# Regrouping the first transfers of a decoder layer: log-decay weights first, decay spreads ahead of the context

## The chip, the cores and the metric

The kernel runs on one core of a Trainium2 chip. The core has a matrix engine (TensorE, PE in the profile, with its weight loads listed as PEld), a vector engine (DVE), an activation engine (ScalarE, ACT), a general engine (GpSimd, POOL) and SyncE (SP), which here only issues transfers. Sixteen DMA engines move data between device memory (HBM) and the core's memory (SBUF); transfers are issued by SP and by ACT. Matrix products land in PSUM, eight banks of which the kernel uses in rotation. The metric is device time in microseconds (us), the median of several executions. One execution was profiled.

## The reference

A post-norm decoder layer on 4 sequences of 1024 tokens with 256 features, in float32, after each of three parts a residual sum and a layer norm:

```python
x = layernorm(x + mamba2(x))             # 16 heads of 16 channels, state 64
x = layernorm(x + cross_attention(x, ctx, mask))   # 16 heads, 77 context tokens
x = layernorm(x + ffn(x))                # 256 -> 1024 -> relu -> 256
```

Inside `mamba2`, for each head, with x the head's 16 channels of the input:

```python
logA = W_logA @ x + b_logA                # one number a token and head
X, Bm, Cm = silu(W_XBC @ x + b_XBC)       # 16, 64 and 64 channels
cum = cumsum(logA)
Y[i] = sum over j <= i of exp(cum[i] - cum[j]) * (Cm[i] . Bm[j]) * X[j]
out = ((W_gate @ x + b_gate) * Y) @ W_out.T + b_out
```

The log-decay weights and biases of the change are `W_logA` and `b_logA`. The context is `ctx`, from which keys and values of the cross attention are made once.

## The kernel before

**Units and stages.** The 4096 tokens are cut into 16 units of 256, each of two chunks of 128. For every unit there are stage A (the Mamba part, with a running state from chunk to chunk inside a sequence), stage B (cross attention) and stage C (the feed-forward part). Every stage is cut into small named jobs. Each job has a place, a number in units of time, from the table `WHEN` or, for units 0, 1 and 15, from `EDGE`. Setup jobs (`s_x`, `s_l`, ...) have places in `WHEN` alone. All jobs are sorted by place and their instructions are issued in that order (L1186 to L1189). Each engine takes its own instructions strictly in this order, so a job that must wait holds up everything behind it on its engine, and a transfer that must wait holds up later transfers of the same issuing engine.

**The opening.** `s_x` (L274) clears the tiles of unit 0's transposed input (`xts[0]`) and of the B and C weights (`w_bc`), and loads them: four slices of `xt` through SP (`load_t`, L248), four slices of `w_bc` and its row of biases through ACT. Then it loads `xu`, a second layout of the transposed input (`load_u`, L240), `w_all` (weights of X, gate and log-decay together) in two halves and the log-decay biases `b_l` in two pieces. `s_l` copies the log-decay columns out of `w_all` into `w_l`; `s_bc` halves `w_bc`; `s_g` loads the X biases and builds `w_x` and `w_g` on GpSimd; `s_x2` and `s_z` clear more tiles there.

`s_c` (L380) loads what the context's keys and values need: `ctxT`, `v_w`, `k_w` (through `packed`, L361, with two GpSimd copies after the load), `v_b`, `k_b` (two loads), the mask twice, and then clears `vz`, the tile of the values, on GpSimd. `s_b` (L403) loads the gate's biases `b_g` in eight small transfers. All of these are issued by SP.

**Unit 0's Mamba part.** `pl` (L585) multiplies `xu` by `w_l`; `cum` (L596) is the running sum over it, with `b_l` as the other operand. `cd` and `ce` (L603, L608) write `cum` to device memory. `dl00`, `dl01`, `dl10` and `dl11` (L616, chunk and half of the heads) read it back, spread over all 128 partitions, 512 KB each: the decay spreads. `ncum` is the negative sum, turned. `ex` (L785) makes exp(cum[i] - cum[j]) on ACT, `sel` (L794) clears the part above the diagonal on GpSimd. `de` (L757) needs both spreads of its chunk.

`pb` (L658) computes B and C on PE, with `xt` and `w_bc`; `th` (ACT) and `bct` (DVE) apply silu; `pg` (L804) is their product on PE, and `st` (L816) multiplies it by the decays on DVE. `px`, `zx`, `thx` and `xz` make X. `pgt` and `gT` (L691, L700) make the gate; `gT` is on ACT and adds `b_g`. `values0` to `values3` (L494) multiply the context of one sequence by `v_w` on PE and add `v_b` into `vz` on DVE.

**The order around the change.** On PE, unit 0 starts with `pb0`, `pl`, `pb1`, `pcum`, `px0`, `pg10`, `px1`, `pgt`, `values0`, then unit 1's `pl` and unit 0's `pg00`, `pg01`. On DVE: the `w_l` copies, the halving of `w_bc`, `bct00`, `cum`, `bct01`, `ncum`, `bct10`, `zx0`, `de0`, `zx1`, `values0`, `xz0`, `bct11`, `st00`. On ACT: its loads, then `th00`, `th01`, `th10`, `th11`, `thx0`, `ex00`, `gT`, `ex01`. On GpSimd: the `b_l` copy, `w_x`, `w_g`, `b_x`, the clears, the copies of `k_w`, the clear of `vz`, `sel00`. On SP: `xt`, `xu`, the loads of `s_c`, `cd`, `ce`, unit 1's `xu`, `dl00`, `dl01`, the loads of `s_b`, `dl11`, `dl10`, then `w_out` in eight pieces.

Of the kernel before, what the change touches and what calls it, by code (L numbers as in the profile page):

```python
# [27 lines left out]
XW = 2 * 64 + 4  # L28
# [5 lines left out]


WHEN = {
    "s_x": -9.9872, "s_l": -9.7484, "s_bc": -8.5276, "s_g": -7.5874, "s_x2": -7.2899,
    "s_z": -5.7593, "s_c": -5.7019, "load_u1": -4.4177, "s_b": -4.0720, "values0": -2.9817,
    "load_u": -2.4239, "pl": -1.9203, "cum": -1.8712, "keys": -1.8678, "s_o": -1.7725,
    "cd": -1.7336, "load_k0": -1.7122, "px1": -1.6221, "ce": -1.5871, "load_t": -1.5843,  # L40
    "values3": -1.5780, "px0": -1.5183, "zx1": -1.5153, "zx0": -1.4952, "pcum": -1.4739,
# [30 lines left out]

EDGE = {
    0: {
        "pb0": -7.2560, "pl": -6.8550, "th00": -6.7669, "bct00": -6.5564, "pb1": -6.2530,
        "cum": -6.1547, "pcum": -5.4565, "th01": -5.3112, "px0": -5.0843, "bct01": -5.0527,
        "cd": -4.9994, "th10": -4.5740, "ce": -4.4923, "ncum": -4.4350, "pg10": -4.3960,
        "dl00": -4.2803, "dl01": -4.2382, "px1": -4.1255, "bct10": -3.8577, "pgt": -3.7592,
        "zx0": -3.6494, "dl11": -3.4590, "de0": -3.3490, "zx1": -3.3017, "th11": -3.2657,
        "thx0": -3.2139, "xz0": -2.9448, "pg00": -2.9088, "bct11": -2.8309, "ex00": -2.7127,  # L80
        "sel00": -2.6115, "dl10": -2.5547, "pg01": -2.3769, "gT": -2.2848, "st00": -2.2420,
        "ptb0": -2.2172, "ex01": -1.9849, "dex0": -1.9659, "bk01": -1.8438, "ec": -1.7085,
        "thx1": -1.7034, "bk00": -1.6781, "de1": -1.5887, "xw0": -1.5820, "sel01": -1.5457,
        "st01": -1.4409, "pc0": -1.2430, "xz1": -1.2245, "ex10": -1.0895, "sn0": -0.9938,
# [87 lines left out]
def decoder_layer_kernel(ctx: ExitStack, tc: tile.TileContext, a: dict, out: bass.AP):  # L172
# [13 lines left out]
    nc = tc.nc  # L186
# [9 lines left out]
    def tile_(shape, tag, name, bufs=2):  # L196
        return sb.tile(shape, F32, tag=tag, name=name, bufs=bufs)
# [17 lines left out]
    xts = [const.tile([P, G, T], F32, name=f"xt_{i}") for i in range(2)]  # L215
# [3 lines left out]
    w_l = const.tile([P, 2, 2 * CH], F32, name="w_l")  # L219
    w_all = const.tile([P, 2, XW], F32, name="w_all")  # L220
    b_x = const.tile([P, 2, 2, 4 * CH], F32, name="b_x")
    b_g = const.tile([P, 2], F32, name="b_g")
    b_l = const.tile([P, 1], F32, name="b_l")
# [16 lines left out]
    def load_u(u):  # L240
        xu = tile_([P, 2, T], "xu", f"xu_{u}", bufs=3)
        nc.sync.dma_start(
            out=xu,
            in_=a["xT"][0:64, :, u * T : (u + 1) * T].rearrange("x (k a) t -> a x k t", a=2),
        )
        xus[u] = xu

    def load_t(u, rs=range(4)):  # L248
        for r in rs:
            nc.sync.dma_start(  # L250
                out=xts[u % 2][32 * r : 32 * r + CH],
                in_=a["xT"][CH * r : CH * r + CH, :, u * T : (u + 1) * T],
            )
# [11 lines left out]
    def setup(name):  # L265
        def put(fn):
            setups.append(name)
            jobs.append((WHEN[name], len(setups) - 100, name, fn))

        return put  # L270

    xgl = a["w_xgl"].rearrange("x (k a) c -> x a k c", a=2)

    @setup("s_x")  # L274
    def _():
        nc.vector.memset(xts[0], 1.0)
        nc.vector.memset(w_bc, 0.0)
        for r in range(4):
            load_t(0, [r])
            own = slice(NS * (r % 2), NS * (r % 2) + NS)  # L280
            nc.scalar.dma_start(
                out=w_bc[32 * r : 32 * r + CH],
                in_=a["w_bc"][CH * r : CH * r + CH, :, :, r // 2, own],
            )
        nc.scalar.dma_start(
            out=w_bc[CH::32], in_=a["w_bc"][64].rearrange("g b q (n s) -> (q n) (g b) s", n=2)
        )
        load_u(0)
        nc.vector.memset(b_l, 0.0)
        nc.vector.memset(w_l, 0.0)  # L290
        for half in range(2):
            nc.scalar.dma_start(out=w_all[64 * half : 64 * half + 64], in_=xgl[0:64, half])
        for k in range(2):
            nc.scalar.dma_start(
                out=b_l[32 * k : 32 * k + 8],
                in_=xgl[64:65, :, k, 128:XW].rearrange("o a r -> r a o"),
            )
        nc.gpsimd.memset(w_x, 0.0)
        nc.gpsimd.memset(w_g, 0.0)
        make_identity(nc, ident)  # L300
        nc.gpsimd.tensor_copy(b_l[64:128], b_l[0:64])

    @setup("s_l")
    def _():
        for half in range(2):
            rows_ = slice(64 * half, 64 * half + 64)
            nc.vector.tensor_copy(
                w_l[rows_, :, 0:8].rearrange("x k (r a) -> x a k r", a=2)[:, half],
                w_all[rows_, :, 128:XW],
            )  # L310
# [876 lines left out]
    with tc.manual_schedule():  # L1187
        for _, _, _, fn in jobs:
            fn()  # L1189
# [77 lines left out]
```

## Time and profile before

Three executions took 698.11, 698.94 and 698.80 us: a median of 698.8. The profiled execution took 698.22, of which its span, from the first to the last instruction, is 696.5 us.

| | busy us | share of the span |
|---|---|---|
| TensorE matmul | 663.4 | 95% |
| TensorE weight load | 526.4 | 76% |
| VectorE | 554.2 | 80% |
| ScalarE | 410.6 | 59% |
| GpSimd | 276.6 | 40% |

| event of the opening | us from the span's start |
|---|---|
| first copy into `w_l`; second | 13.68; 14.64 |
| first matmul (`pb0`) | 15.32 |
| first activation (`th00`) | 18.26 |
| `cum` of unit 0 | 20.09 |
| `cd` issued; `dl00` and `dl01` issued | 20.53; 22.17 to 24.12 |
| `values0` on TensorE | 26.23 to 27.26 |
| second half of `de0` | 33.35 |
| `st00` | 36.09 |

In the lines that follow, "engine line waited for" lists give the waiting engine and line, what ended the wait, the total in us, how many times, and the longest. Lines of the timeline give the start, the length, the engine, the source line, the operation, out<-in, and in brackets the engine's idle time before it and what ended it. ACTq and SPq are the sequencers of ACT and SP, which issue transfers. In the line of a stretch stand its bounds and length, the busy time of PE, PEld, DVE, ACT and POOL with the numbers of instructions, the granted clock of TensorE, the busy share of the DMA engines, and GB/s.

### The profile page before, as it was taken

The numbers are of one execution on the slowest core, as the hardware profiler recorded it, in microseconds if no ns is written. First come the engines' busy times: TensorE is split into PE (matmuls) and PEld (weight loads), VectorE is DVE, ScalarE is ACT, GpSimd is POOL, SyncE is SP. The second block draws the span as 40 slices with busy tenths as digits, with TensorE's granted clock in tenths as the row PEclk, the third lists the DMA queues.
The fourth block names the chain that finished last, engine by engine and source line by source line (L and its number), as shares of the span: only waits on it lengthen the run. The fifth ranks groups of instructions, "written<-read, shape, count | busy, mean of one in ns | idle before, by whom it ended". The sixth has DMA issues, their size and how long they took to land.

```text
span 696.5 us, 19937 instructions
## 1 busy us (share of the span) xinstructions
PE 663.4 (95%) x7968; PEld 526.4 (76%) x7968; DVE 554.2 (80%) x1336; ACT 410.6 (59%) x1091; POOL 276.6 (40%) x448
## 2 busy tenths in 40 slices
PE   1689999999999999999999999999999999999996
PEld 0466777878878787887878788787878788787785
DVE  1388899688888798979888788988878897887653
ACT  0476896647485674838566683837658483853210
POOL 0443445243435354334443435435434443533222
PEclk9988999999999999999999999999999999999999
DMA  4375547032232303223230423223130331100001
GB/s 113 95 182 173 182 142 236 23 114 79 77 122 63 116 22 120 88 85 122 85 108 22 155 85 113 93 85 114 52 119 33 119 95 62 48 1 17 16 1 46
DMA packets 40440, 63.08 MB, mean 91 GB/s; under 512 B 6095, under 2 KB 29340, under 8 KB 40348
## 3 DMA queue, kind: packets, MB, share of 16 engines
q1 hardware_dynamic: 38880, 61.40, 28.5%
q8 instruction: 63, 1.03, 0.6%
q10 hardware_dynamic: 1468, 0.41, 0.3%
q14 instruction: 29, 0.24, 0.1%
HBM read 55.50 MB, written 6.29 MB: 89 GB/s over the span
## 4 chain that ended last, share of the span: by engine, by line
PE 90%; DVE 4%; DMA 3%; SPq 1%; ACT 0%; issue 0%; POOLq 0%; POOL 0%; DVEq 0%
PE pf L1162 17%; PE ph L1135 16%; PE pg L811 9%; PE pb L666 5%; PE pe L1044 5%; PE pa L1069 4%; PE po_a L942 4%; PE pq L972 4%; PE py L915 4%; PE po_b L1105 4%; PE pm L997 3%; PE py L854 2%; PE ptb L832 2%; PE pc L869 2%; PE px L728 2%; PE pgt L695 2%
## 5 line engine op out<-in xcount | busy, mean ns | idle before, releaser
L789 ACT ACTIVATE dl<-dl,ncum 128x128 f32<-128x128 f32 x512 | 156.1, 397 | 8.0 <-DVE de L761 8.0
L797 POOL TENSOR_SCALAR_AFFINE_SELECT dl<-dl 128x1024 f32<-128x1024 f32 x64 | 69.9, 1103 | 136.4 <-ACT dl L789 136.4
L1162 PE MATMUL pf<-w,hT 128*128 128x256 f32 x512 | 122.8, 385 | 0.0
L1135 PE MATMUL ph<-T_c,w 128*128 128x256 f32 x512 | 121.6, 383 | 0.0
L1055 ACT ACTIVATE es<-pe,mb 77x512 f32<-77x512 f32 x128 | 76.9, 679 | 59.2 <-PE pe L1044 58.1
L1135 PEld LDWEIGHTS ph<-T_c,w 128*128 128x128 f32 x512 | 93.9, 190 | 18.0 <-issue 5.4
L1162 PEld LDWEIGHTS pf<-w,hT 128*128 128x128 f32 x512 | 93.0, 190 | 14.3 <-issue 2.1
L821 DVE TENSOR_TENSOR dl<-pg,dl 128x512 f32<-128x512 f32 x128 | 81.8, 681 | 7.4 <-PE pg L811 4.8
L686 DVE SCALAR_TENSOR_TENSOR bct<-th,pb 128x512 f32<-128x512 f32 x128 | 80.9, 673 | 4.6 <-ACT th L678 4.3
L678 ACT ACTIVATE th<-pb 128x512 f32<-128x512 f32 x128 | 69.7, 592 | 20.9 <-PE pb L666 14.5
L811 PE MATMUL pg<-bct 64*128 64x128 f32 x1024 | 72.6, 287 | 2.8 <-DVE zx L736 2.5
L811 PEld LDWEIGHTS pg<-bct 64*128 64x128 f32 x1024 | 64.0, 194 | 11.7 <-DVE bct L686 3.4
L843 ACT COPY bk<-ptb 128x512 f32<-128x512 f32 x56 | 30.9, 586 | 65.7 <-PE ptb L832 65.7
L1008 DVE TENSOR_REDUCE maxes<-pm 128x4 f32<-128x308 f32 x128 | 52.0, 469 | 16.6 <-PE pm L997 16.6
L666 PE MATMUL pb<-xt,w_bc 17*64 17x256 f32 x1024 | 44.1, 410 | 15.6 <-DVE w_bc L315 15.3
L1151 ACT ACTIVATE hT<-ph,b 128x256 f32<-128x256 f32 x64 | 26.7, 471 | 52.3 <-PE ph L1135 51.3
L1087 POOL TENSOR_TENSOR on<-at,rec 128x256 f32<-128x256 f32 x32 | 20.6, 643 | 69.5 <-DVE rec L1082 69.4
L666 PEld LDWEIGHTS pb<-xt,w_bc 17*64 17x64 f32 x1024 | 23.8, 138 | 31.0 <-DVE w_bc L315 15.3
L936 POOL TENSOR_TENSOR yg<-ya,gT 128x256 f32<-128x256 f32 x28 | 20.5, 732 | 51.9 <-DVE ya L929 34.3
L1146 DVE TENSOR_SCALAR hT<-ph,b 128x256 f32<-128x256 f32 x64 | 27.8, 478 | 15.6 <-PE ph L1135 15.6
L904 ACT COPY state<-pts 64x128 f32<-64x128 f32 x56 | 14.4, 257 | 38.5 <-PE pts L894 38.1
L1044 PE MATMUL pe<-qm,kT 32*77 32x256 f32 x512 | 35.2, 389 | 0.0
(124 smaller groups left out, 1190.5 us busy)
## 6 DMA issues: line engine op xcount, KB each, us to landing
dl<-cd SPq DMA_DIRECT2D x64, 512.0 KB
xt<-in_xT_dram SPq DMA_DIRECT2D x64, 64.0 KB
xu<-in_xT_dram SPq DMA_DIRECT2D x16, 256.0 KB
xk<-in_x_dram SPq DMA_DIRECT2D x16, 256.0 KB
ec<-ce SPq DMA_DIRECT2D x16, 256.0 KB
out_dram<-r SPq DMA_DIRECT2D x32, 128.0 KB
w<-in_w_dram SPq DMA_DIRECT2D x2, 1024.0 KB
cd<-cum SPq DMA_DIRECT2D x16, 64.0 KB
```

Source lines behind the costliest of these rows:

```text
L666: nc.tensor.matmul(pbs[r][64 * half : 64 * half + 64, bc, :], lhsT=w_bc[rs, 2 * gk + half, bc, :], rhs=xt[rs, 2 * gk + half, :], start=Tru ...
L678: nc.scalar.activation(th, s[f"pb{gk}"][r], AF.Tanh)
L686: nc.vector.scalar_tensor_tensor(t, s[f"th{gk}{r}"], 1.0, s[f"pb{gk}"][r], ALU.add, ALU.mult)
L789: nc.scalar.activation(dl[:, h, :], dl[:, h, :], AF.Exp, bias=s["ncum"][:, 2 * c + k, h : h + 1],)
L797: nc.gpsimd.affine_select(out=dl, in_=dl, compare_op=ALU.is_ge, fill=0.0, base=0, pattern=[[0, 8], [1, P]], channel_multiplier=-1,)
L811: nc.tensor.matmul(pgs[half][:, r, :], lhsT=t[lo : lo + 64, 0, cs], rhs=t[lo : lo + 64, 1, cs], start=True, stop=True,)
L821: nc.vector.tensor_tensor(d, v[f"pg{k}"][half], d, ALU.mult)
L1008: nc.vector.tensor_reduce(mx[:, :, at : at + 2], s[f"pm{c}"][r].rearrange("p k a s -> p a k s"), AX.X, ALU.max, negate=True,)
L1044: nc.tensor.matmul(pes[r][:, par, :], lhsT=kT[rs, gp, par, bs], rhs=s["qm"][rs, par, gp, :], start=True, stop=True,)
L1055: nc.scalar.activation(e, s[f"pe{gp}"][r], AF.Exp, bias=mb[:, b : b + 1], scale=CH**-0.5)
L1135: nc.tensor.matmul(ph[:, j, :], lhsT=w1[:, k, f * P : (f + 1) * P], rhs=s["xT"][:, k, :], start=(k == 0), stop=(k == 1),)
L1162: nc.tensor.matmul(pf, lhsT=s["hT"][:, f, c * P : (c + 1) * P], rhs=w2[:, f, :], start=(f == 0), stop=(f == FF // P - 1),)
```

## The change

- The clear of `xts[0]` moves from DVE to GpSimd, ahead of GpSimd's other clears; `b_l` and `w_l` are cleared before `w_bc`.
- `w_all` is loaded by one transfer instead of two halves, first on ACT's queue; `load_u(0)` and the two loads of `b_l` come next, ahead of the slices of `xt` and `w_bc`.
- The copy of `b_l` into its upper half moves from GpSimd to DVE, at the head of `s_l`.
- `pl` and `cum` of unit 0 are placed ahead of `pb0`; on DVE this puts `cum` right behind the halving of `w_bc`.
- `dl10` and `dl11` of unit 0 are placed right behind `dl00` and `dl01`. `s_c` moves from before `cd` to behind the four spreads; `s_b` stays just behind it. On SP the order is now `xu`, `xt`, `cd`, `ce`, unit 1's `xu`, four spreads, the loads of `s_c`, the loads of `s_b`, `w_out`.

```diff
--- before.py
+++ after.py
@@ -34,8 +34,8 @@
 
 
 WHEN = {
-    "s_x": -9.9872, "s_l": -9.7484, "s_bc": -8.5276, "s_g": -7.5874, "s_x2": -7.2899,
-    "s_z": -5.7593, "s_c": -5.7019, "load_u1": -4.4177, "s_b": -4.0720, "values0": -2.9817,
+    "s_x": -9.9872, "s_l": -9.7400, "s_bc": -8.5276, "s_g": -7.5874, "s_x2": -7.2899,
+    "s_z": -5.7593, "load_u1": -4.4177, "s_c": -4.0500, "s_b": -4.0000, "values0": -2.9817,
     "load_u": -2.4239, "pl": -1.9203, "cum": -1.8712, "keys": -1.8678, "s_o": -1.7725,
     "cd": -1.7336, "load_k0": -1.7122, "px1": -1.6221, "ce": -1.5871, "load_t": -1.5843,
     "values3": -1.5780, "px0": -1.5183, "zx1": -1.5153, "zx0": -1.4952, "pcum": -1.4739,
@@ -72,13 +72,13 @@
 
 EDGE = {
     0: {
-        "pb0": -7.2560, "pl": -6.8550, "th00": -6.7669, "bct00": -6.5564, "pb1": -6.2530,
-        "cum": -6.1547, "pcum": -5.4565, "th01": -5.3112, "px0": -5.0843, "bct01": -5.0527,
+        "pl": -7.2700, "cum": -7.2620, "pb0": -7.2560, "th00": -6.7669, "bct00": -6.5564,
+        "pb1": -6.2530, "pcum": -5.4565, "th01": -5.3112, "px0": -5.0843, "bct01": -5.0527,
         "cd": -4.9994, "th10": -4.5740, "ce": -4.4923, "ncum": -4.4350, "pg10": -4.3960,
-        "dl00": -4.2803, "dl01": -4.2382, "px1": -4.1255, "bct10": -3.8577, "pgt": -3.7592,
-        "zx0": -3.6494, "dl11": -3.4590, "de0": -3.3490, "zx1": -3.3017, "th11": -3.2657,
-        "thx0": -3.2139, "xz0": -2.9448, "pg00": -2.9088, "bct11": -2.8309, "ex00": -2.7127,
-        "sel00": -2.6115, "dl10": -2.5547, "pg01": -2.3769, "gT": -2.2848, "st00": -2.2420,
+        "dl00": -4.2803, "dl01": -4.2382, "dl10": -4.2000, "dl11": -4.1900, "px1": -4.1255,
+        "bct10": -3.8577, "pgt": -3.7592, "zx0": -3.6494, "de0": -3.3490, "zx1": -3.3017,
+        "th11": -3.2657, "thx0": -3.2139, "xz0": -2.9448, "pg00": -2.9088, "bct11": -2.8309,
+        "ex00": -2.7127, "sel00": -2.6115, "pg01": -2.3769, "gT": -2.2848, "st00": -2.2420,
         "ptb0": -2.2172, "ex01": -1.9849, "dex0": -1.9659, "bk01": -1.8438, "ec": -1.7085,
         "thx1": -1.7034, "bk00": -1.6781, "de1": -1.5887, "xw0": -1.5820, "sel01": -1.5457,
         "st01": -1.4409, "pc0": -1.2430, "xz1": -1.2245, "ex10": -1.0895, "sn0": -0.9938,
@@ -273,8 +273,17 @@
 
     @setup("s_x")
     def _():
-        nc.vector.memset(xts[0], 1.0)
+        nc.gpsimd.memset(xts[0], 1.0)
+        nc.vector.memset(b_l, 0.0)
+        nc.vector.memset(w_l, 0.0)
         nc.vector.memset(w_bc, 0.0)
+        nc.scalar.dma_start(out=w_all, in_=a["w_xgl"][0:64].rearrange("x (k a) c -> a x k c", a=2))
+        load_u(0)
+        for k in range(2):
+            nc.scalar.dma_start(
+                out=b_l[32 * k : 32 * k + 8],
+                in_=xgl[64:65, :, k, 128:XW].rearrange("o a r -> r a o"),
+            )
         for r in range(4):
             load_t(0, [r])
             own = slice(NS * (r % 2), NS * (r % 2) + NS)
@@ -285,23 +294,13 @@
         nc.scalar.dma_start(
             out=w_bc[CH::32], in_=a["w_bc"][64].rearrange("g b q (n s) -> (q n) (g b) s", n=2)
         )
-        load_u(0)
-        nc.vector.memset(b_l, 0.0)
-        nc.vector.memset(w_l, 0.0)
-        for half in range(2):
-            nc.scalar.dma_start(out=w_all[64 * half : 64 * half + 64], in_=xgl[0:64, half])
-        for k in range(2):
-            nc.scalar.dma_start(
-                out=b_l[32 * k : 32 * k + 8],
-                in_=xgl[64:65, :, k, 128:XW].rearrange("o a r -> r a o"),
-            )
         nc.gpsimd.memset(w_x, 0.0)
         nc.gpsimd.memset(w_g, 0.0)
         make_identity(nc, ident)
-        nc.gpsimd.tensor_copy(b_l[64:128], b_l[0:64])
 
     @setup("s_l")
     def _():
+        nc.vector.tensor_copy(b_l[64:128], b_l[0:64])
         for half in range(2):
             rows_ = slice(64 * half, 64 * half + 64)
             nc.vector.tensor_copy(
```

## The prediction

> **What bounds the kernel now.** I read the busy line first, then what TensorE (PE) waited for over the whole span, then stretches, then the opening engine by engine.
>
> ```profile
> PE 663.4 (95%) x7968; PEld 526.4 (76%) x7968; DVE 554.2 (80%) x1336; ACT 410.6 (59%) x1091; POOL 276.6 (40%) x448
> ```
>
> ```profile
> PE pb L666 <- DVE w_bc L315: 15.3, 1, 15.3
> PE pl L591 <- DMA xu<-in_xT_dram: 3.7, 1, 3.7
> PE pg L811 <- DVE zx L736: 2.5, 1, 2.5
> PE ptb L832 <- DVE dl L821: 2.0, 1, 2.0
> ```
>
> ```profile
> 70.00:680.00 610.00, 608.45 (x7462) 486.19 (x7461) 507.48 (x1215) 376.62 (x1003) 250.88 (x398) 1.00 0.27 86
> ```
>
> From 70 to 680 us PE is busy 608.45 of 610 us at full clock. So a microsecond lost or won before about 50 us is lost or won at the end, one for one: there is no slack later to absorb it. Of PE's long waits, 21.5 us lie before 34 us: one for w_bc and two for unit 0's decay spreads and what is queued around them. The chain and the vector engine (DVE) show which:
>
> ```profile
> 4.88 10.25 DMA xu<-in_xT_dram
> 15.15 1.81 DMA b_l<-in_w_xgl_dram
> ...
> 23.69 9.64 DMA dl<-cd
> 33.35 0.07 DVE de L761
> ```
>
> ```profile
> 33.35 0.17 DVE L761 TENSOR_TENSOR de<-dl,ncum 128x8 f32<-128x8 f32 x1 [1.04 <-DMA dl<-cd]
> 33.44 0.41 DVE L736 TENSOR_TENSOR zx<-px,b_x 128x256 f32<-128x256 f32 x1
> 33.77 0.41 DVE L504 TENSOR_TENSOR vz<-pv,v_b 77x256 f32<-77x256 f32 x1
> 34.10 0.48 DVE L750 SCALAR_TENSOR_TENSOR xz<-thx,zx 128x128 f32<-128x128 f32 x2
> 34.51 1.27 DVE L686 SCALAR_TENSOR_TENSOR bct<-th,pb 128x512 f32<-128x512 f32 x2
> ```
>
> The restart is paced by dl01 at 33.3 us. Behind `de` stand `vz` (values0) and the last `bct`, in order; from 34.5 to 51 DVE hardly stops (15.05 of 17.09 us). The start of that `bct`, 34.51 us, is my milestone. values0 costs nothing now because its inputs landed early, and gT's biases just fit:
>
> ```profile
> 24.88 0.78 POOL L367 COPY kv_w<-kv_w 128x256 f32<-128x256 f32 x2
> 25.56 1.84 POOL L401 MEMSET vz<- 77x2048 f32 x1
> 34.87 1.09 POOL L797 TENSOR_SCALAR_AFFINE_SELECT dl<-dl 128x1024 f32<-128x1024 f32 x1 [7.46 <-ACT dl L789]
> ```
>
> ```profile
> 35.12 0.84 ACT L704 ACTIVATE gT<-pgt,b_g 128x256 f32<-128x256 f32 x2 [0.33 <-DMA b_g<-in_w_xgl_dram]
> ```
>
> Last, SyncE's (SP) own waits:
>
> ```profile
> SPq L375 <- DMA kv_w<-in_v_w_dram: 4.5, 1, 4.5
> SPq L408 <- DMA xu<-in_xT_dram: 4.3, 1, 4.3
> ```
>
> k_b's load needs nothing of v_w, nor b_g's of xu. Yet they wait: the DMA records name eight completion semaphores, used in turn over SP and ACT together, and a ninth transfer is not issued until the first has landed.
>
> **What the skill says, and the trace.** "DMA: Bandwidth & Descriptors", section "Why a DMA increments its semaphore by 16 and not by 1": a transfer runs on the largest k up to 16 that divides the slowest dimension of both its sides, on the lowest-numbered k engines. xu's source starts with a = 2, so k = 2. The trace agrees: the packets of unit 1's xu, 256 of 1 KB, run from 23.0 to 30.3 us, at best 23 in 0.5 us (two engines, 43.5 ns each), while the other 14 engines finish dl00 by 27.2. Same page, "Queues, rings and completion order": an engine consumes one ring in order and alternates between SP's and ACT's rings. It agrees: dl00's share on engines 0 and 1 lands only at 32.06, after xu, and dl01's at 33.34. "ScalarE: Activation LUTs", "What ACT_TABLE_LOAD costs", gives 1.283 us; measured 1.28.
>
> **The change, step by step.**
>
> 1. *w_all as one transfer, first, with load_u(0) beside it.* Instead of two half loads on 16 engines, its source starts with a = 2, the form of xu: k = 2, the same two engines. Each gets 128 packets of 1 KB (43.5 ns) and 128 of 528 B (28 to 31 ns in this trace): 5.6 + 3.8 = 9.4 us. Engines pass the opening barrier near 0.75 us, so both issue at about 1.0; xt's first packets came 1.5 us after issue, so the two engines work from 2.5 to 11.9 and the pair lands at about 12.3. Before, w_all landed at 13.6 and 14.6. The xt memset on GpSimd (1.0 us, its twin at L338) is hidden under this; so is the DVE copy of b_l (0.18 us), and the biases follow w_all in ACT's ring.
>
> 2. *The ninth and tenth transfers wait for the first two.* In order of issue the first eight are w_all, xu, two b_l and about three xt and one w_bc; next come w_bc rows (ACT) and the last xt (SP). Both find a semaphore held by w_all or xu, so ACT stands at L281 until about 12.4. Queued behind on ACT: three w_bc rows (0.65 us each), the w_bc bias row (1.10), two b_x (0.45), the table load. The bias row issues at about 14.5 and lands some 3.1 us later (before: 5.50, first landings at 8.65 and 9.14): 17.65. Then the w_bc multiply (0.43): pb0 at 18.1, against 15.32. th00 moves from 18.26 to about 20.5. This 2.8 us is covered: before, PE ran out of work at 27.3 and stood until 33.9.
>
> 3. *pl and cum moved ahead of pb0.* cum follows the multiply on DVE: 18.15 to 18.56, against 20.09 to 20.50. cd issues at 18.6 instead of 20.53: a gain of 1.9 us. The barrier of bct and the GpSimd copy before cum are gone.
>
> 4. *Four spreads in a row.* Before, cd's issue to dl01's landing was 12.8 us, mostly xu of unit 1, which still precedes the spreads. Same again: 31.4. The other 14 engines now carry 2 MB rather than 1 MB, so xu runs longer at the slow rate seen at 26 to 28 us (15 to 16 packets in 0.5 us, against 23): its last 96 packets cost 0.9 us more: 32.3. Alone this gains 1.0 us. dl10 and dl11 follow on engines 0 and 1, each 8 packets of 4 KB at 163 ns: 1.3 us, so 33.6 and 34.9. Unit 0 did not want them before 40 us.
>
> 5. *Context behind them.* On engines 0 and 1: ctxT 16 packets at 57 ns, v_w 16 at 48 ns, k_w 16 at 86 ns: 0.9 + 0.8 + 1.4 us. v_w has landed at 36.6, k_w at 38.0. values0 stands on PE ahead of unit 1's pl and of pg00, so these wait until 36.6. GpSimd stands at the k_w copies until 38.0; behind them the vz memset ends 2.55 us later by the rows above (24.88 to 27.40), at 40.55, and sel00 waits behind that. DVE's `vz` waits for the memset: 40.6, and the last `bct` starts 0.74 us later at 41.3. Against 34.51: **+6.8 us**.
>
> 6. *b_g last.* Its eight transfers wait, each in turn, for ctxT, v_w, k_w, v_b, both k_b, mrow and mcol. mcol itself waits for dl11 (34.9), so the last b_g issues at about 40.5 and lands 1.5 to 2 us later: gT at about 42.3, +7.2 us. ex01 and sel01 are queued behind it on ACT and GpSimd, but the product that needs them ran at 41.26, 5.2 us after st00, with about 1 us of slack, which covers the 0.4 us. w_out and cd of unit 1 follow on SP some 5 to 6 us later than now: within the same shift.
>
> Sum: milestone +6.8 us, nothing given back later. The profiled execution took 698.22 (span 696.5 and 1.7 around it), so 705.0; the median shown, 698.8, is 0.6 above it: **705.6 us**. A move within 0.2% (1.4 us) can't be told from none.
>
> Unknown prices, from both ends: the pair at step 1 between 11 and 13 us (engines that overlap two rings, or xu's slow first packets again, 0.75 us): -1.3 to +0.7. The spreads and context on engines 0 and 1 while the others are still busy: 4 KB packets at up to 235 ns rather than 163 ns give up to +2.3 over four spreads; taken: none beyond the 0.9 in step 4. Context packets faster than seen: at most -0.5.
>
> **The rivals.**
>
> *The waiting w_bc row holds xu's semaphore, and xu ends first* (0.2). When the 8 packets of w_bc's bias row shared these engines with xu, ACT's ring got few turns: they took from 7.5 to 11.0 us. If xu so wins, it lands near 9.5, ACT goes on then, and pb0 starts at about 15.2, cum 2.9 us earlier than in my sum: +3.9, 702.7 us. Against: w_all's own rows, later, got one turn for every two of xu.
>
> *No wait on ACT* (0.1). If the semaphores fall otherwise, w_bc lands right behind w_all, at about 12.9, and cum ends at 14.2: +2.5, 701.3 us.
>
> *The context stays hidden, faster* (0.07). Then only the spreads count: step 4's 1.0 us, so 697.8 us, or down to 693.5 with cum at 14.2. It decides at the GpSimd copies, L367: the gain stands if k_w lands by about 30 us, 2.6 us of copies and memset before dl01. For it: the 14 other engines could be through by 34. Against: engines 0 and 1 carry xu first, then everything in order.
>
> *Congestion to the end* (0.13): the 235 ns packets and a slow b_g chain: +9 to +10, 708 us.
>
> **How the numbers follow.** The likeliest case has 0.5: 705.6, own range 704 to 707.5. Range over the cases: 700.6 to 708.6; outside it lie the faster case and part of the congested one. Slower by over 0.2%: 0.5 + 0.2 + 0.13 and most of the 0.1: 0.88. Within 0.2%: 0.05. Faster: 0.07.
>
> **What would show it.** Right: w_l's copies at 12 to 13 us; an ACT issue at L281 standing from about 3 to 12; pb0 near 18 and cum before 19; de of dl01 near 32; then PE, DVE and GpSimd all idle until 37 to 41, with `vz` waiting for L401, the k_w copies for their DMA and gT for b_g. Wrong: k_w landed by 30 us would overturn steps 5 and 6; w_bc landed by 13 us overturns step 2; w_all spread over 16 engines overturns step 1.

## The result and the profile after

The changed kernel took 704.26 us (median of four executions, 703.87 to 704.71), the kernel before 698.56 on the same occasion: a ratio of 1.0082, with a 95% interval of 1.0065 to 1.0100. The prediction was 705.6. The span of the profiled execution went from 696.5 to 703.0 us.

The busy line of the page, and the waits of TensorE (PE) over the whole span, after. Lines of `kernel.py` from the middle on are one lower than before: L498 was L499.

```profile
PE 666.8 (95%) x7968; PEld 529.0 (75%) x7968; DVE 553.7 (79%) x1336; ACT 410.6 (58%) x1091; POOL 277.2 (39%) x448
```

```profile
PE pl L590 <- DMA xu<-in_xT_dram: 13.5, 1, 13.5
PE pv L498 <- DMA kv_w<-in_v_w_dram: 7.7, 1, 7.7
PE pb L665 <- DMA b_x<-in_w_xgl_dram: 3.2, 1, 3.2
PE ptb L831 <- DVE dl L820: 1.8, 1, 1.8
```

The waits for unit 1's xu (3.7 us) and for `zx` (2.5 us) are gone; a single wait of 7.7 us at values0, for `v_w`, stands in their place. The opening's wait of 15.3 us is split: `pl` runs at 13.5 us, and then PE waits again, until 17.4, for `pb0`. (The list names `b_x` for that wait; what `pb0` needs is w_bc, whose halving ended at 17.32.) From 75 to 690 us nothing is given back (a stretch: bounds, length, busy time of PE, PEld, DVE, ACT, POOL, clock, DMA share, GB/s):

```profile
75.00:690.00 615.00, 613.43 (x7483) 490.01 (x7482) 511.79 (x1223) 379.56 (x1011) 252.28 (x399) 1.00 0.27 86
```

ACT's and VectorE's (DVE) timelines of the opening, after (lines left out at the dots):

```profile
3.85 10.78 ACTq L290 DMA_DIRECT2D w_bc<-in_w_bc_dram  x4
```

```profile
16.89 0.43 DVE L314 TENSOR_SCALAR w_bc<-w_bc 128x512 f32<-128x512 f32 x1 [5.36 <-DMA w_bc<-in_w_bc_dram]
17.23 0.41 DVE L598 TENSOR_TENSOR_SCAN cum<-b_l,pl 128x128 f32<-128x128 f32 x1
...
31.49 0.17 DVE L760 TENSOR_TENSOR de<-dl,ncum 128x8 f32<-128x8 f32 x1 [1.07 <-DMA dl<-cd]
31.57 0.42 DVE L735 TENSOR_TENSOR zx<-px,b_x 128x256 f32<-128x256 f32 x1
39.51 0.42 DVE L503 TENSOR_TENSOR vz<-pv,v_b 77x256 f32<-77x256 f32 x1 [7.52 <-POOL vz L400]
39.85 1.02 DVE L749 SCALAR_TENSOR_TENSOR xz<-thx,zx 128x128 f32<-128x128 f32 x2
40.79 1.27 DVE L685 SCALAR_TENSOR_TENSOR bct<-th,pb 128x512 f32<-128x512 f32 x2
```

Everything the change aimed at came earlier: `cum` by 2.9 us, dl01 (the second line of `de`) by 1.9 us. Then `vz` waits 7.5 us for the clear of its tile on GpSimd, and the last `bct` starts at 40.79 instead of 34.51: 6.3 us late, and the span is 6.5 us longer. GpSimd and ACT show the two chains behind that:

```profile
37.00 0.73 POOL L366 COPY kv_w<-kv_w 128x256 f32<-128x256 f32 x2 [13.97 <-DMA kv_w<-in_k_w_dram]
37.68 1.80 POOL L400 MEMSET vz<- 77x2048 f32 x1
39.44 1.08 POOL L796 TENSOR_SCALAR_AFFINE_SELECT dl<-dl 128x1024 f32<-128x1024 f32 x1
```

```profile
40.95 0.84 ACT L703 ACTIVATE gT<-pgt,b_g 128x256 f32<-128x256 f32 x2 [8.05 <-DMA b_g<-in_w_xgl_dram]
```

The reader is to see that GpSimd stood 14 us at the two copies of `k_w` and that the clear of `vz` and `sel00` come straight behind; and that `gT` waited 8 us for the gate's biases, a wait of 0.33 us before.

### The profile page after: what moved, and what is told of

Read it like the earlier page. It is cut to its first block, busy times and chain, and to the rows that moved or that the text cites. A ratio compares the mean times of both kernels' runs of the same rounds, so it can differ in the third digit from the quotient of the medians.

```text
span 703.0 us, 19936 instructions
## 1 busy us (share of the span) xinstructions
PE 666.8 (95%) x7968; PEld 529.0 (75%) x7968; DVE 553.7 (79%) x1336; ACT 410.6 (58%) x1091; POOL 277.2 (39%) x448
## 3 DMA queue, kind: packets, MB, share of 16 engines
q1 hardware_dynamic: 38880, 61.40, 28.1%
q8 instruction: 63, 1.03, 0.6%
## 4 chain that ended last, share of the span: by engine, by line
PE 89%; DVE 4%; issue 2%; DMA 2%; POOL 1%; ACTq 0%; POOLq 0%; ACT 0%; DVEq 0%
PE pf L1161 16%; PE ph L1134 16%; PE pg L810 9%; PE pb L665 5%; PE pe L1043 5%; PE pa L1068 4%; PE po_a L941 4%; PE pq L971 4%; PE py L914 4%; PE po_b L1104 4%; PE pm L996 3%; PE py L853 2%; PE ptb L831 2%; PE pc L868 2%; DMA xu<-in_xT_dram 2%
```

## The experiments

Twelve kernels, in three groups, each compared with the kernel before on the same chip. That kernel scattered there between 697 and 707 us, so I read the ratio to it, with its 95% interval, ahead of the median, and the events of the trace for where the time goes. The table gathers them (us; `st01` is VectorE's second product with decays, the last event of the opening that both chains lead to). From `st01` to the end of the span it is 655.2 us in the kernel before, 655.4 in the changed one and between 653.6 and 658.4 in the others, so `st01` stands for the whole to within a few us. The events are those of one profiled execution each, and some of these lie off the median: 3.4 us above it for opening only, 3.0 for no biases, 2.8 for opening only with both in halves, and 1.8 below it for the changed kernel with `w_all` in halves.

| kernel | cum | dl01's de | last bct | st01 | ratio (interval) |
|---|---|---|---|---|---|
| before | 20.09 | 33.35 | 34.51 | 41.26 | 1 |
| changed | 17.23 | 31.49 | 40.79 | 47.55 | 1.0082 (1.0065 to 1.0100) |
| changed, third group | 17.64 | 31.94 | 41.28 | 47.69 | 1.0060 (1.0035 to 1.0085) |
| opening only | 20.36 | 33.52 | 34.67 | 41.46 | 0.9980 (0.9958 to 1.0001) |
| moves only | 17.60 | 31.63 | 40.89 | 47.81 | 1.0055 (1.0026 to 1.0084) |
| context ahead | 19.42 | 33.91 | 35.06 | 44.41 | 1.0029 (1.0016 to 1.0043) |
| clear of vz early | 17.43 | 31.73 | 39.35 | 46.52 | 1.0051 (1.0035 to 1.0068) |
| no biases | 16.93 | 31.55 | 41.38 | 48.48 | 1.0047 (1.0030 to 1.0063) |
| no biases, clear early | 17.20 | 31.42 | 38.57 | 44.19 | 1.0000 (0.9982 to 1.0019) |
| before, xu in halves | 17.87 | 26.74 | 27.89 | 34.33 | 0.9880 (0.9839 to 0.9920) |
| changed, w_all in halves | 12.25 | 27.58 | 36.97 | 42.99 | 1.0005 (0.9982 to 1.0028) |
| changed, xu in halves | 11.03 | 20.55 | 32.22 | 39.15 | 0.9923 (0.9900 to 0.9945) |
| opening only, both in halves | 10.98 | 23.01 | 24.16 | 30.35 | 0.9820 (0.9791 to 0.9848) |
| the same, small loads late | 11.01 | 20.21 | 22.26 | 32.34 | 0.9802 (0.9771 to 0.9832) |

**Which part makes the loss: the opening or the moves?** The opening alone puts the places of `s_c`, `s_b`, `dl10` and `dl11` back; the moves alone leave `s_x` and the places of `pl` and `cum` as before.

```diff
-    "s_z": -5.7593, "load_u1": -4.4177, "s_c": -4.0500, "s_b": -4.0000, "values0": -2.9817,
+    "s_z": -5.7593, "s_c": -5.7019, "load_u1": -4.4177, "s_b": -4.0720, "values0": -2.9817,
-        "dl00": -4.2803, "dl01": -4.2382, "dl10": -4.2000, "dl11": -4.1900, "px1": -4.1255,
+        "dl00": -4.2803, "dl01": -4.2382, "px1": -4.1255,
...
+        "zx0": -3.6494, "dl11": -3.4590, "de0": -3.3490,
...
+        "sel00": -2.6115, "dl10": -2.5547, "pg01": -2.3769,
```

> The changed kernel with the four spreads, the context and the gate's biases put back to their old places; only the opening is regrouped (w_all in one transfer, xu and b_l first, pl and cum ahead of pb0). Theory (the loss is the context and its GpSimd work behind the spreads): the loss goes away. cum stays near 17.5 to 18.5, dl01 lands near 31.5 to 32.5, the last bct of unit 0 starts near 33 instead of 40.8: 696.5 to 698.5 us. Rival (the regrouped opening, with w_all and xu on two engines and w_bc late, makes the loss): 702 us or more.

Measured: 697.5 us, ratio 0.998. The loss is gone, as the theory had it.

> The kernel before with its old opening and only the places of dl10, dl11, the context and the gate's biases changed. Theory: nearly the whole loss, since cum comes at about 17.5 here too (the context no longer crowds xu and w_all), and the last bct starts at 40 to 42: 703.5 to 706 us. Rival (the opening makes the loss): 697 to 700 us.

Measured: 704.38 us, ratio 1.0055, with the last `bct` at 40.89 and `gT` waiting 8.6 us. The moves alone hold the loss. One expected value of the opening-only kernel missed: `cum` came at 20.36, not 17.5 to 18.5. Its VectorE waited 8.4 us for w_bc, and the list names a transfer of the context:

```profile
DVE w_bc L314 <- DMA k_b<-in_k_b_dram: 8.4, 1, 8.4
```

The name is misleading. `k_b` only uses the semaphore of another w_bc row again; what landed last was w_bc's own row of biases, issued at 14.73 and landed at 19.79, 5.1 us later, while the context's `v_w` and `k_w` were moving. In the changed kernel the same row took 1.9 us (14.67 to 16.60). SP's waits show the landing: the mask's load, which takes this row's semaphore next, waits for w_bc and is issued at 19.80:

```profile
SPq L396 <- DMA w_bc<-in_w_bc_dram: 1.3, 1, 1.3
```

So the earlier `cum` of the changed kernel is no gift of the regrouped opening. It comes from taking the context out of the way: with the old opening and the context moved, `cum` is at 17.60; with the new opening and the context ahead, at 19.4 to 20.4.

**Four spreads in a row, without the late context.** The changed kernel with `s_c` and `s_b` back (the first two lines of the diff above), `dl10` and `dl11` still early.

> The changed kernel with the context's and the gate's loads back ahead, and the four spreads of unit 0 still in a row. Theory: de0 paces the milestone again; only the gate's biases are late, by the two further spreads (1.3 us each), and about 1 us of that is covered: 697 to 699.5 us, within 1.5 us of the opening-only kernel. Rival (four spreads in a row are what costs): 701 us or more.

Measured: 701.05 us, ratio 1.0029: outside the theory's range and at the rival's lower bound. The last `bct` is at 35.06, as the theory had it, but `st01` is 2.95 us later than in the opening-only kernel, with this wait on ACT:

```profile
38.25 0.84 ACT L703 ACTIVATE gT<-pgt,b_g 128x256 f32<-128x256 f32 x2 [2.91 <-DMA b_g<-in_w_xgl_dram]
```

The biases are 2.9 us late (two spreads more ahead of them), and TensorE feels it: it waits for `gT`, and then for a copy behind it on ACT.

```profile
39.14 1.12 PE L831 MATMUL ptb<-ident,bct 64*128 64x64 f32 x16 [0.57 <-ACT gT L703]
40.18 1.22 PE L727 MATMUL px<-w_x,xu 128*128 128x128 f32 x4
41.20 0.42 PE L635 MATMUL pcum<-ident,cum 128*128 128x128 f32 x1
42.04 1.99 PE L498 MATMUL pv<-kv_w,ctxT 128*77 128x256 f32 x4 [0.42 <-ACT bk L842]
```

So values1 (the last line) starts at 42.04, 2.0 us after the 40.05 of the opening-only kernel. The last microsecond is another thing: its four matmuls take 1.99 us here and 1.03 there, because TensorE's granted clock is 0.50 from 34 to 44 us here and only from 36.6 to 39.9 there. My "about 1 us of slack" was counted at the product that needs `sel01`; TensorE, which waits for ACT as well, had less. The rival is right in part: four spreads in a row cost some 2 us at values1 through the biases queued behind them, and through their own consumers at most the 0.4 us by which dl01 is later. Whether the late biases also caused the longer stretch of half clock is not shown.

**Two chains: k_w to vz, and b_g to gT.** First the clear of `vz` moved from the end of `s_c` to `s_z`, ahead of the copies of `k_w`:

```diff
         for t in xzs + states + maxes:
             nc.gpsimd.memset(t, 0.0)
+        nc.gpsimd.memset(vz, 1.0)
...
-        nc.gpsimd.memset(vz, 1.0)
```

> The changed kernel with one move: GpSimd clears vz with its other tiles, ahead of the copies of k_w instead of behind them. Theory (k_w, copies, clear, then vz on VectorE is the chain that ends last): vz then starts when the first values are out of TensorE, at about 37.7 instead of 39.5, and the end moves by the same 1.8 us: 702 to 703 us. Rival (the wait of gT for the gate's biases, 8.05 us on ScalarE, sets the pace): no change, 704 to 704.6 us.

Measured: 702.99 us, ratio 1.0051; the interval overlaps that of the changed kernel's second measurement (1.0060), so the gain in time is not clear of noise. In the trace the last `bct` moved by 1.4 us, to 39.35, `st01` by 1.0. VectorE's next wait comes a little later, for `sel01`, which hangs on `gT` and `ex01`:

```profile
38.09 0.42 DVE L503 TENSOR_TENSOR vz<-pv,v_b 77x256 f32<-77x256 f32 x1 [5.86 <-POOL kv_w L367]
...
46.52 1.29 DVE L820 TENSOR_TENSOR dl<-pg,dl 128x512 f32<-128x512 f32 x2 [0.96 <-POOL dl L796]
```

The first line names the copies of `k_w`, which ended at 38.03, but `vz` does not need them: in the kernel with both edits (below) it starts at 37.83, before they end at 38.18. What it waited for is values0 on TensorE, which started at 36.03, when `v_w` had landed, and ended at 38.0. So behind the clear stands the next part of the late context: `v_w` alone keeps `vz` about 4 us later than it was in the kernel before (33.77).

Then, in the third group, the biases' loads left out altogether (`b_g` cleared instead, so the gate has no bias in these two kernels), alone and with the early clear:

```diff
+        nc.vector.memset(b_g, 0.0)
...
-        for half in range(2):
-            for r in range(4):
-                at = 32 * r + CH * half
-                nc.sync.dma_start(
-                    out=b_g[at : at + CH],
-                    in_=xgl[64, half, :, 64 + CH * r : 64 + CH * r + CH].rearrange("k c -> c k"),
-                )
+        pass
```

> The changed kernel itself, beside the next two on one chip: 0.7 to 0.9% over the kernel before, about 704.3 us.

> The changed kernel without the eight loads of the gate's biases: b_g is cleared to zero at the start instead, so the gate's bias is left out of the computation. gT then waits for nothing. Theory (k_w, copies, clear of vz, vz is the chain that ends last, and the biases run beside it): 0 to 0.8 us less than the changed kernel, with the last bct of unit 0 still near 40.8. Rival (gT's 8 us wait sets the pace): 3 us less or more.

> The same, with the clear of vz moved ahead of the copies of k_w as well. Theory (two chains side by side; with the first shortened by 1.4 us the second took back 0.4 to 1 us): 1.6 to 2.4 us less than the changed kernel, and VectorE's second product no longer waits for sel01. If the biases never mattered, the same as with the early clear alone: 1.2 to 1.5 us less.

Measured: the changed kernel 704.74 us (1.0060, a little under the 0.7% expected), without biases 703.72 (1.0047), without biases and with the early clear 700.91 (1.0000). Without the biases alone the last `bct` stays at 41.38 and the difference of 0.0013 in the ratio, 0.9 us, lies inside both intervals: the chain over the context and `vz` is enough to hold the time. (This kernel's `st01` of 48.48 is not to be compared: its profiled execution had TensorE's clock at 0.50 until 48.6 us.) With both edits the gain is 0.006, 4.2 us, about twice what I expected; `st01` moved by 3.5 us. VectorE's two products then follow without a wait for the decays:

```profile
40.27 1.29 DVE L815 TENSOR_TENSOR dl<-pg,dl 128x512 f32<-128x512 f32 x2 [0.43 <-PE pg L805]
...
44.19 1.28 DVE L815 TENSOR_TENSOR dl<-pg,dl 128x512 f32<-128x512 f32 x2
```

From the last `bct` to `st01` it is 5.6 us here, 6.8 in the changed kernel and 6.75 in the kernel before. That does not make ACT too late in the kernel before. There `sel01` was through at 40.33, 0.9 us ahead of `st01`, which stood behind a `vz` waiting for TensorE:

```profile
39.24 1.09 POOL L797 TENSOR_SCALAR_AFFINE_SELECT dl<-dl 128x1024 f32<-128x1024 f32 x1
40.91 0.42 DVE L504 TENSOR_TENSOR vz<-pv,v_b 77x256 f32<-77x256 f32 x1 [0.48 <-PE pv L499]
41.26 1.27 DVE L821 TENSOR_TENSOR dl<-pg,dl 128x512 f32<-128x512 f32 x2
```

A rival that no run separates is TensorE's clock. It was granted at 0.50 until 38.5 us in the kernel before, four microseconds past its last `bct`, and until 45.0 in the changed one, again four past it, but here only until 39.9, one past it. How much of the 1.2 us, and so of the 4.2, is the clock's is open.

**The two engines.** `xu` of every unit in two transfers of 64 partitions, in the kernel before and in the changed one; `w_all` in its old halves in the changed one; both, in the opening-only kernel. The Trainium skill, "DMA: Bandwidth & Descriptors", section "Rules for kernel authors", says that an outermost dimension of a size c below 16 confines the whole transfer to at most c engines; `w_all` and `xu` lead with 2. The four runs agree, with dl01 8.4 us behind `cd` instead of 12.8 in the first and `pl` at 10.90 instead of 13.52 in the third:

```diff
-        nc.sync.dma_start(
-            out=xu,
-            in_=a["xT"][0:64, :, u * T : (u + 1) * T].rearrange("x (k a) t -> a x k t", a=2),
-        )
+        halves = a["xT"][0:64, :, u * T : (u + 1) * T].rearrange("x (k a) t -> a x k t", a=2)
+        for half in range(2):
+            nc.sync.dma_start(out=xu[64 * half : 64 * half + 64], in_=halves[half])
```

```diff
-        nc.scalar.dma_start(out=w_all, in_=a["w_xgl"][0:64].rearrange("x (k a) c -> a x k c", a=2))
+        for half in range(2):
+            nc.scalar.dma_start(out=w_all[64 * half : 64 * half + 64], in_=xgl[0:64, half])
```

> The kernel before with one edit: xu of every unit is loaded by two transfers of 64 partitions each instead of one whose source starts with a = 2. Theory (xu sits on two of the sixteen engines and holds everything behind it on those two): its first load lands near 8.5 instead of 15.1, and dl01 follows cd by about 8 us instead of 12.8, so the last bct of unit 0 starts near 27 instead of 34.5: 690 to 692.5 us. Rival (the spreads are slow by their own bytes): dl01 still 11 us or more after cd, gain from the opening only: 695.5 us or more.

Measured: 690.84 us, ratio 0.9880. dl01 lands 8.4 us after `cd` is issued (18.32) instead of 12.8:

```profile
26.74 0.17 DVE L760 TENSOR_TENSOR de<-dl,ncum 128x8 f32<-128x8 f32 x1 [1.01 <-DMA dl<-cd]
```

> The changed kernel with the same edit. Theory: w_all is alone on its two engines and lands near 6.5, w_bc follows, cum comes near 12.5, and the row of spreads, context and biases runs on sixteen engines: k_w lands near 28 to 29 and vz starts near 31.5 instead of 39.5: 694 to 697.5 us, still behind the kernel before with the same edit, since the order is unchanged. Rival (the order alone makes the loss, whatever the engines): the gap to the kernel before stays and the time is 702 us or more.

Measured: 695.45 us, ratio 0.9923. `cum` and the last `bct` both come earlier; the order's own loss stays: the last `bct` is 4.3 us behind the kernel before with the same edit, though `cum` is 6.8 us ahead of it, and the wait on the clear of `vz` is longer than ever:

```profile
30.93 0.42 DVE L502 TENSOR_TENSOR vz<-pv,v_b 77x256 f32<-77x256 f32 x1 [8.38 <-POOL vz L399]
```

> The changed kernel with w_all in its two old halves on sixteen engines, first in the queue as in the change. Theory: w_all lands near 4, xu alone takes its two engines and lands near 10 to 11 instead of 13.4, so the w_bc row that waits for xu goes on 2.5 to 3 us earlier and everything behind it too: 701 to 702.5 us. Rival (w_all in one transfer costs nothing): 704 to 704.6 us.

Measured: 701.34 us, ratio 1.0005 beside 1.0060 to 1.0082 for the changed kernel. `xu` alone on its engines lets `pl` run at 10.90 instead of 13.52, and the last `bct` moves by 3.8 us. The intervals lie apart: `w_all` in one transfer does cost.

> The regrouped opening with the old places of spreads, context and biases, and with both w_all and xu in two transfers of 64 partitions. Theory: w_bc lands near 10.5, cum comes near 11 to 12, dl01 lands near 20 to 21 and the last bct of unit 0 starts near 21.5 to 23.5: 685.5 to 689 us. If the loads of the context, ahead of cd on SP, hold cd up, cum to cd grows and the time is 689 to 692 us.

Measured: 687.54 us, ratio 0.9820: better than both kernels. `cum` is at 10.98, but `cd` is issued only at 14.16; SP's waits name `k_w`, whose semaphore `cd` needs (2.2 us; here the trace has the semaphore's last update, `k_w`'s, at 14.07). So dl01 came at 23.0, later than the 20 to 21 expected. The last try takes the small loads of the context out from between; their new step `s_c2` has the place -4.1000, behind dl01 and ahead of `s_b`:

```diff
         packed(ctx_["k_w"], "k_w")
+        nc.gpsimd.memset(vz, 1.0)
+
+    @setup("s_c2")
+    def _():
+        v_b = ctx_["v_b"]
         nc.sync.dma_start(out=v_b, in_=a["v_b"].partition_broadcast(S))
...
-        nc.gpsimd.memset(vz, 1.0)
```

> The regrouped opening with old places and both loads in halves, and one edit more: v_b, k_b and the two masks are issued after dl01 instead of ahead of cd. Theory (SP stands at these small loads, which wait for semaphores held by k_w and others, while cum is ready): cd follows cum at once, near 11.5 instead of 14.2, dl01 lands 2 to 2.7 us earlier, and the time is 1.5 to 2.7 us under the kernel without the edit: 684.5 to 686.5 us. Rival (the spreads are then held by the context's bytes on the same engines): no gain, 687 to 688 us.

Measured: 687.25 us, ratio 0.9802. `cd` went at 11.45 and dl01 landed 2.8 us earlier, as expected, and the last `bct` came 1.9 us earlier. But the biases are again behind more transfers: `gT` waits 3.4 us instead of 0.8, TensorE waits 2.5 us for `gT` instead of 0.3, and `st01` is 2.0 us later; TensorE's clock was 0.50 from 26 to 32.6 us as well, and 1.00 there without the edit. The gain of 1.5 to 2.7 us that I expected did not come. Whether it is better than the kernel without the edit is open; the intervals overlap.

## Why the prediction was right

*What bounds.* Right: the last `bct` moved by 6.3 us, `st01` by 6.3, the span by 6.5, the median by 5.7.

*Step 1 (the pair on two engines).* Right in kind: `w_all` and `xu` stand on the same two engines, and each in halves lands much earlier. The order of landing was not as I had it. I let both end at 12.3; a transfer that waited for `w_all` was issued at 10.51 and one that waited for `xu` at 13.41. In the packets, `w_all` starts at 2.3 us and `xu` only at 4.06, 3.3 us after its issue; then they share evenly, 15 packets each in half a microsecond. The rival in which `xu` ends first had it the wrong way round.

*Step 2 (the ninth and tenth transfers).* Right: ACT stood at L290 from 3.85 to 14.63, at a row of w_bc that waited for `xu`, and the bias row was issued at 14.67 (14.5 predicted). That this figure is so close is luck: the wait ended at 13.41, a microsecond later than I had it, but only two rows of w_bc were left to issue and not three. The bias row then landed 1.9 us after its issue, not the 3.1 that I took from a busier moment, so w_bc was multiplied at 16.89 and `pb0` ran at 17.42 (18.1). That delay was covered, as said: PE was through with what it had at 28 us.

*Step 3.* `cum` at 17.23, `cd` at 17.68: a gain of 2.9 us where I had 1.9, the same microsecond. The moves-only kernel, with `cum` at 17.60, shows that the context's absence brings this gain; the prediction credited the new order of `cum`. Right in size, wrong in the cause.

*Step 4.* From `cd` to dl01's `de` 13.8 us; predicted 13.7. Right.

*Step 5 (k_w, copies, clear, vz).* Right, and the main term: copies at 37.0 (38.0), `vz` at 39.51 (40.6), last `bct` +6.3 (+6.8). The microsecond is step 2's. That the late context is the cause is shown by the two orders (opening only, moves only). Within it the early clear moves the last `bct` by 1.4 us and no more, because values0, late by `v_w`, ends just behind; so the copies and the clear are the last 1.4 us of the 6.3, and `v_w` alone would hold most of the rest. The prediction had `v_w` as well, at 36.6 (values0 ran at 35.78).

*Step 6 (the biases).* `gT` at 40.95 (42.3), in the right place. The third `b_g` went at 36.97, just after `k_w` landed, as listed, so this chain hangs on `k_w` too. The cover of about 1 us was there for `sel01`: it ended 0.9 us ahead of `st01` before, and 1.4 ahead in the changed kernel. TensorE was left out of it: with the context ahead, a `gT` 2.9 us late put values1 back by 2.0 us. In the changed kernel the biases cost little of their own only because step 5 is as late.

*Size.* The forecast is 1.3 us above the median, the microsecond of step 2 and a little scatter.

## What to carry to other kernels

When work is moved forward in a transfer queue, follow what falls behind it to its first consumer on every in-order engine: here the landings of `v_w` and `k_w`, through four matmuls, a small copy and a clear, held VectorE for 7.5 us, and eight transfers of a few bytes held ACT for 8, although the spreads that were moved arrived sooner. Look at a transfer's outermost dimension before its place in the queue: two transfers of 64 partitions in place of one with a leading 2 were worth 1.2% in the unchanged order, more than any reordering tried. And when one wait is removed, look for the second chain that ends within a microsecond of it; the early clear and the biases gave little alone and 4 us together, part of which may be TensorE's clock. Last, check the name that a list gives for a wait: where several waits end together or semaphores are used again, it can be the wrong one, as with `k_b` for w_bc's row of biases and the copies of `k_w` for values0.

## What the hardware showed that I had not expected

- Two transfers on the same two engines did not share them from the start: the packets of `xu`, issued at 0.80 us together with `w_all`, began 1.75 us after those of `w_all`. Why was not tried.
- In the changed kernel PE had nothing to do from 28.1 to 35.8 us. Its granted clock fell to 0.50 at 31.35, 3.3 us into that gap, and stayed there until 45.0, 9 us after PE had resumed; the four matmuls of values0 took 1.96 us, against 1.03 before. The Trainium skill, "TensorE: Matmul & The Clock Gate", section "Part 1: The HAM clock gate", states half rate after some 3.4 us of idling, and this agrees with it. At values0 it cost nothing, since `vz` waited longer for GpSimd, and from the last `bct` to `st01` no more than in the kernel before, whose clock was 0.50 from 31.65 to 38.48 (6.76 us and 6.75). In the kernel with `xu` in halves and the old order PE's gap was 1.7 us and the clock stayed at 1.00 until 43.5. The stretch of the changed kernel:

```profile
35.00:45.00 10.00, 8.28 (x61) 6.33 (x61) 5.39 (x15) 3.27 (x11) 4.16 (x6) 0.50 0.19 44
```

- Loads that need nothing of each other are tied by the completion semaphores: in the changed kernel a row of w_bc waited for `xu` until 13.41, and in the opening-only kernel with both in halves `cd` waited for `k_w` until 14.16, 2.8 us after `cum` was done.
